# A graph layer's last edges: one run of six groups, or two groups after each of three mixing products

## The chip, the cores and the metric

The kernel runs on one core of a Trainium2 chip (trn2). The metric is the device time of one execution in microseconds (us); the time before is the median of three runs. One further execution was recorded by the hardware profiler, and every view below is of that one.

## The reference

One layer over a graph of 10000 nodes with 512 features and 160000 edges sorted by their target (`dst`), all in float32:

```
xn = layernorm(x)
gnn = relu(segment_sum((xn @ W)[src] * edge_weight, dst) + bias)
q, k, v = xn @ w_qkv.T                 # 8 heads of 64
q = softmax(q, over features) / 8 ; k = softmax(k, over nodes)
mix = layernorm(concat_heads(q @ (k.T @ v)) @ w_out.T) * gamma
x = x + gnn + mix
t = layernorm(x)
router: mean over nodes -> 11 logits -> top 2 -> weight of each of 6 experts
x = x + sum_e weight_e * (gelu(t @ W1_e + b1_e) @ W2_e + b2_e)
```

## The kernel before

The nodes go in 20 chunks (`NCH`): 19 of 512 nodes and a last one, number 19, of 272. A chunk lies on up to 128 partitions, r, with four nodes (`SUB`) on each; a product of the matmul engine takes one of the four, s = 0 to 3. The last chunk has r = 68.

**Edges.** Since segment_sum is linear, the kernel sums normalised rows first and multiplies by W after. `edges_in` (L573) lets GpSimd (POOL) gather rows of the source nodes, 128 at a time, by an indirect DMA (L584), and has VectorE (DVE) make the matrix `sel` that places and weighs them (L590, L592). `edges_summed` (L596) does four matmuls of 128x32 by 128x512 on TensorE (PE, L602) into a PSUM tile `pm` of a pool with two buffers, lets ScalarE (ACT) copy it into `part` (L605, three buffers), and starts a DMA of 256 KB from ACT's queue to `part_d` in memory (L606). In this part of the kernel, that is one group of edges: four gathers, four matmuls, one copy, one DMA. `edges_to(n)` (L689) does groups until n are done, issuing gathers until more than `ahead` tiles of 128 edges are held (`LATE`, 4, in this part); `work(us)` and `put_out` spread groups between products by a pace. There are `NQ` groups in all. Now and then `carry` (L673, issue at L674) adds the second half of some windows' sums to the next window's by one accumulating DMA on POOL's queue.

**Rows.** `attention(c)` (L1041) computes the mixing branch of chunk c: four products `po` (called by `times`, L209), a copy of each to `ot` (L1055) on ACT, statistics, and two DVE steps that finish it. It runs three chunks ahead (`MIXED`). The loop over the chunks then gathers the summed rows (`gathered`, L1016, an indirect DMA on POOL at L1020, which needs the edges of these rows and their carry), transposes them on PE (`pt`, L201) with copies on ACT (`aT`, L203), multiplies by W (`pg`, L209), adds bias and relu and the mixing branch on DVE (L1104, L1105), stores the rows (`x_d`, L1106) from SyncE's (SP's) queue, and takes statistics.

**The tail.** The change stands at c = 17, the third chunk from the end. There `all_edges_in` (L1006) finishes the edges that are left: six groups, one after the other. It then issues the last carry, closes the edges' pools, issues the loads of the first chunk for the experts (`rows_in(0)`, L328, four DMAs on SP) and of the experts' weights (three small ones on ACT's queue, and 17 on SP, L305 and L306). The gathers for chunks 18 and 19 follow, and then attention for chunk 19: products s = 0, 1, 2, then by `beside()` the 16 transposes of chunk 17, then s = 3. Because the pools of the edges are closed, `put_out` does nothing there any more. Small products `pst` (L337) and ACT's normalising (L351) prepare the first chunk for the experts, DVE transposes it (L367), and pg of chunks 17, 18 and 19 follow. After chunk 17, `sums_of_weights` has DVE form sums of W1's blocks (L226 to L229), which the experts' first products (`px`, L243) use; these fill the rest of the kernel.

PE runs in the order in which the program is written (`manual_schedule`). The orders of ACT and DVE are set by a scheduler from the dependences. POOL's and SP's instructions stand in one order each, and every engine runs its own in order.

Of the kernel before, what the change touches and what calls it, by code (L numbers as in the profile page):

```python
# [20 lines left out]
SUB = 4  # L21
# [12 lines left out]
PRODUCT = 0.83  # L34
# [22 lines left out]
def gps_layer_kernel(  # L57
# [22 lines left out]
    KB = D // P  # L80
# [16 lines left out]
    NCH = len(chunks)  # L97
# [50 lines left out]
    NQ = -(-NW // GROUP)  # L148
# [239 lines left out]
    with ExitStack() as ph:  # L388
# [184 lines left out]
        def edges_in(i):  # L573

            t0, batch = tiles_of(i)
            n = min(GROUP * batch, NET - t0)
            m = [None] * n
            for j in range(batch):
                four_of = pools["m"].tile([P, GROUP, D], F32, name="msg")
                for h in range(GROUP):  # L580
                    k = h * batch + j
                    if k < n:
                        m[k] = four_of[:, h, :]
                        nc.gpsimd.indirect_dma_start(  # L584
                            out=m[k], out_offset=None, in_=xn_d,
                            in_offset=bass.IndirectOffsetOnAxis(ap=src_sb[:, t0 + k : t0 + k + 1], axis=0))
            sel = pools["w"].tile([P, 2 * GROUP, WIN], F32, name="sel", bufs=6)
            if n < GROUP * batch:
                nc.vector.memset(sel[:, n:, :], 0.0)
            nc.vector.tensor_tensor(sel[:, :n], iota_w[:, None, :].to_broadcast([P, n, WIN]),  # L590
                                    place[:, t0 : t0 + n, None].to_broadcast([P, n, WIN]), ALU.is_equal)
            nc.vector.tensor_tensor(sel[:, :n], sel[:, :n],  # L592
                                    w_sb[:, t0 : t0 + n, None].to_broadcast([P, n, WIN]), ALU.mult)
            return batch, m, sel
# [89 lines left out]
        done = [0, 0.0]  # L684
# [4 lines left out]
        def edges_to(stop):  # L689
            while done[0] < stop:  # L690
                i = done[0]
                while sum(len(m) for _, m, _ in held["edges"]) <= ahead[0] and i + len(held["edges"]) < NQ:
                    held["edges"].append(edges_in(i + len(held["edges"])))
                edges_summed(i, *held["edges"].pop(0))
                done[0] += 1
                while carried and carried[0][0] == i:
                    carried.pop(0)[1]()

        def work(us):

            done[1] += us
            if not pools:

                normal_rows(int(done[1] / EARLY_TOTAL * (NCH + 1)) + 4 - len(normal))
                return
            edges_to(groups_of(int(done[1] / pace[0])))
# [150 lines left out]
        for c, (_, r) in enumerate(chunks):  # L857
# [31 lines left out]
            else:  # L889
# [4 lines left out]
                for s in range(SUB // 2):  # L894
                    first = seven(ek, qt, s, r, xnT, xs, (wk, wq), kq_sum, lambda n: work(n * KH * PRODUCT))
# [110 lines left out]
        def all_edges_in():  # L1006
            edges_to(NQ)
            carry(CARRIES[-1], NW - 1)
            assert not carried
            pools.clear()  # L1010
            edge_ctx.close()
            io_f["in"] = ctx.enter_context(tc.tile_pool(name="f_in", bufs=1, reuse_waits="tile"))
            held["first_rows"] = rows_in(0)
            experts_weights()

        def gathered(c):  # L1016
            r = chunks[c][1]
            n_rows = far_enough(c)
            at = io.tile([P, SUB, D], F32, name="at", tag="at" if c < NCH - 1 else "qT")
            nc.gpsimd.indirect_dma_start(  # L1020
                out=at[:r].rearrange("p s d -> p (s d)"), out_offset=None, in_=by_four[: n_rows // SUB, :],
                in_offset=bass.IndirectOffsetOnAxis(ap=row_of[:r, c : c + 1], axis=0))
            return at
# [11 lines left out]
        def put_out(us):  # L1035
            if pools:
                work(us)

        ats = []

        def attention(c, beside):  # L1041


            r = chunks[c][1]
            qT, xt = held.pop("last") if c == NCH - 1 else (queries_in(c), rows_again(c))
            ot = io.tile([P, SUB, D], F32, name="ot", bufs=MIXED + 2)
            for s in range(SUB):
                if s == SUB - 1:
                    beside()
                po = psum.tile([P, D], F32, name="po", tag="ps")  # L1050
                times(po, qT, s, r, mix)
                put_out(KB * PRODUCT)
                if c == s == 0:
                    ats.append(gathered(0))
                nc.scalar.copy(ot[:r, s, :], po[:r, :])  # L1055
            mv = small.tile([P, SUB, 2], F32, name="mv")
            row_stats(ot, r, mv)
            for s in range(SUB):
                nc.vector.scalar_tensor_tensor(ot[:r, s, :], ot[:r, s, :], mv[:r, s, 0:1],
                                               gamma_b[:r], op0=ALU.subtract, op1=ALU.mult)  # L1060
                nc.vector.scalar_tensor_tensor(ot[:r, s, :], ot[:r, s, :], mv[:r, s, 1:2],
                                               xt[:r, s, :], op0=ALU.mult, op1=ALU.add)
            return ot

        mixed = [attention(c, lambda: None) for c in range(MIXED)]
        for c, (_, r) in enumerate(chunks):
            ot, at = mixed.pop(0), ats.pop(0)
            aT = io.tile([P, KB, SUB * P], F32, name="aT", bufs=1)

            if c == NCH - 3:  # L1070
                all_edges_in()
                ats += [gathered(c + 1), gathered(c + 2)]

            def nodes_rows():
                transposed(aT, at, r, psum, "ps", by_act=range(KB))

            if c + MIXED < NCH - 1:
                mixed.append(attention(c + MIXED, nodes_rows))
            elif c == NCH - 3:
                mixed.append(attention(NCH - 1, nodes_rows))  # L1080
            else:
                nodes_rows()
            if c < NCH - 3:
                ats.append(gathered(c + 1))
            if c == NCH - 4:
                held["last"] = queries_in(NCH - 1), rows_again(NCH - 1)

            if c == NCH - 3:
                io_f["squares"] = io_f["in"].tile([P, P // SQ, P], F32, name="squares")
                for b in range(P // SQ):  # L1090
                    nc.vector.tensor_copy(
                        io_f["squares"][:, b].rearrange("k (g t) -> k g t", t=SQ),
                        ident[:, None, b * SQ : (b + 1) * SQ].to_broadcast([P, P // SQ, SQ]))
                xn = held.pop("first_rows")
                st = small.tile([P, P // SQ, 1, SUB, 2], F32, name="st_sq", bufs=1)
                stats_of_squares(st, 0)
                for step in normalising(0, xn, st[:, :, 0]):
                    step()
                turn = turned_in(0, rows_turned(0, xn))
            for s in range(SUB):  # L1100
                po = psum.tile([P, D], F32, name="pg", tag="ps")
                times(po, aT, s, r, wg)
                put_out(KB * PRODUCT)
                nc.vector.tensor_tensor(po[:r, :], po[:r, :], bias_b[:r], ALU.add)  # L1104
                nc.vector.scalar_tensor_tensor(ot[:r, s, :], po[:r, :], 0.0, ot[:r, s, :], op0=ALU.max, op1=ALU.add)  # L1105
            nc.sync.dma_start(x1_d[c], ot[:r])  # L1106
            mv = stats2[:, c]
            row_stats(ot, r, mv)

            if c == NCH - 1:  # L1110
                normalize(wg, ot, r, mv)

            nc.vector.scalar_tensor_tensor(mv[:r, :, 0], mv[:r, :, 0], -1.0, mv[:r, :, 1],
                                           op0=ALU.mult, op1=ALU.mult)
            if c < NCH - 1:
                for s in range(SUB):
                    nc.vector.scalar_tensor_tensor(xsum[:r], ot[:r, s, :], mv[:r, s, 1:2], xsum[:r],
                                                   op0=ALU.mult, op1=ALU.add)
                moved = small.tile([P, 1], F32, name="moved")
                nc.vector.tensor_reduce(moved[:r], mv[:r, :, 0], axis=AX.X, op=ALU.add)  # L1120
                nc.vector.tensor_tensor(msum[:r], msum[:r], moved[:r], ALU.add)
            if c == NCH - 3:
                sums_of_weights()
# [350 lines left out]
```

## Time and profile before

| | us |
|---|---|
| median of 3 runs | 3495.81 |
| lowest and highest | 3495.39, 3496.99 |
| profiled execution | 3479.47 |
| its span (first to last instruction) | 3477.7 |
| PE busy | 3259.1 |
| DVE busy | 1764.0 |
| POOL busy | 1323.8 |
| ACT busy | 831.0 |
| mean granted TensorE clock | 0.968 of full speed |

Times in a trace are counted from the first instruction, so the profiled execution ends at 3477.7. An engine's busy time is the sum of its instructions; what matters for a change is which engine waits, where, and for whom. "x24" behind a line of the timeline counts instructions as the profiler records them: a float32 matmul of the program has two records, so a group of edges (four matmuls) is x8, and a product of four matmuls is also x8. The number in brackets is idle time just before, with the instruction that ended it by the semaphore events ("issue" is none that the profile shows, "remote" one that it cannot name).

### The profile page before, as it was taken

To read this page: it belongs to the slowest core of one execution; us is meant where nothing else is said; L and a number is where in the kernel's file an instruction comes from. 1 tells how busy PE (TensorE), PEld (TensorE's weight loads), DVE (VectorE), ACT (ScalarE), POOL (GpSimd) and SP (SyncE) were. 2 spreads that over 40 slices of the span, in tenths; PEclk is the share of its full clock that TensorE was granted. 3 is DMA by queue.
4 is the path that set the end of the run, shared out by engine and by line. 5 is a ranking of instruction groups with operands and counts; after the bars stand their busy time and mean duration, and the time that the engine had idled before them with its cause. 6 is when DMAs were issued, how large, how long until landed. Compare 5 with 4: busy or idle time off the path is not lost. (4 is left out here: it accounts for less than half of the span.)

```text
span 3477.7 us, 35221 instructions
## 1 busy us (share of the span) xinstructions
PE 3259.1 (94%) x12819; PEld 1917.7 (55%) x12819; DVE 1764.0 (51%) x3902; ACT 831.0 (24%) x1674; POOL 1323.8 (38%) x1421
## 2 busy tenths in 40 slices
PE   6899999998999889999999989999999999999998
PEld 3343433333333333333333336888888888888886
DVE  6654544444445435555555557455445445544542
ACT  5322211121122112222221223222222222222221
POOL 3366666666666657767767630000000000000000
PEclk9999999999999979999999999999999999999999
DMA  9677777777767879989899882122121212212111
GB/s 389 239 224 250 226 251 251 256 225 225 239 218 246 256 278 324 322 313 323 312 321 326 291 256 72 53 81 58 52 85 49 61 54 80 57 53 84 50 38 38
DMA packets 216728, 654.33 MB, mean 188 GB/s; under 512 B 34425, under 2 KB 74361, under 8 KB 188831
## 3 DMA queue, kind: packets, MB, share of 16 engines
q0 software_dynamic: 104096, 354.29, 32.2%
q1 hardware_dynamic: 69992, 175.33, 15.3%
q10 hardware_dynamic: 42452, 122.31, 9.2%
q8 instruction: 105, 1.72, 0.2%
q14 instruction: 83, 0.68, 0.1%
HBM read 491.21 MB, written 166.63 MB: 189 GB/s over the span
## 5 line engine op out<-in xcount | busy, mean ns | idle before, releaser
L584 POOL DMA_INDIRECT msg<-xn_d,src_sb x1250 | 1241.6, 993 | 611.0 <-issue 333.9
L602 PE MATMUL pm<-msg,sel 128*32 128x512 f32 x2504 | 356.1, 616 | 40.2 <-issue 34.3
L209 PE MATMUL po<-G,qT 128*128 128x512 f32 (+1 forms) x640 | 305.9, 616 | 24.7 <-issue 23.2
L912 PE MATMUL pc<-xn,ek 128*128 128x512 f32 (+1 forms) x640 | 309.4, 634 | 10.5 <-issue 7.7
L209 PE MATMUL pg<-wq,aT 128*128 128x512 f32 (+1 forms) x640 | 296.4, 608 | 9.7 <-issue 9.0
L605 ACT COPY part<-pm 128x512 f32<-128x512 f32 x217 | 127.0, 585 | 712.7 <-remote 254.6
L209 PEld LDWEIGHTS po<-G,qT 128*128 128x128 f32 (+1 forms) x640 | 117.7, 192 | 202.7 <-issue 195.5
L602 PEld LDWEIGHTS pm<-msg,sel 128*32 128x32 f32 x2504 | 65.8, 110 | 291.9 <-issue 261.1
L209 PEld LDWEIGHTS pg<-wq,aT 128*128 128x128 f32 (+1 forms) x640 | 115.1, 188 | 190.4 <-issue 177.8
L912 PEld LDWEIGHTS pc<-xn,ek 128*128 128x128 f32 (+1 forms) x640 | 125.7, 204 | 170.0 <-issue 158.5
L243 PE MATMUL px<-xnT,w_sb 128*128 128x256 f32 (+1 forms) x800 | 203.2, 377 | 9.1 <-DVE u L1291 9.0
L243 PE MATMUL p<-kq_sum,xs_b 128*128 128x512 f32 (+1 forms) x432 | 201.2, 600 | 2.7 <-issue 2.4
L243 PE MATMUL px<-w_sb,hh 128*128 128x256 f32 (+1 forms) x800 | 185.7, 379 | 0.0
L243 PE MATMUL py<-xs,w_sum 128*128 128x256 f32 (+1 forms) x800 | 185.0, 374 | 0.0
L166 DVE BATCH_NORM_STATS2 st<-ot 128x6 f32<-128x512 f32 (+1 forms) x160 | 110.1, 689 | 137.6 <-issue 74.3
L243 PE MATMUL py<-w_sum,hh 128*128 128x256 f32 (+1 forms) x800 | 179.2, 379 | 0.0
L590 DVE TENSOR_TENSOR sel<-iota_w,place 128x128 f32<-128x128 f32 (+2 forms) x217 | 74.5, 344 | 194.5 <-remote 74.2
L243 PEld LDWEIGHTS px<-xnT,w_sb 128*128 128x128 f32 x800 | 149.5, 191 | 32.5 <-DVE u L1291 13.0
L243 PEld LDWEIGHTS px<-w_sb,hh 128*128 128x128 f32 (+1 forms) x800 | 150.0, 188 | 22.7
L243 PEld LDWEIGHTS py<-w_sum,hh 128*128 128x128 f32 (+1 forms) x800 | 150.0, 188 | 22.7
L243 PEld LDWEIGHTS py<-xs,w_sum 128*128 128x128 f32 x800 | 149.4, 190 | 19.6
L243 PE MATMUL p<-wk,xnT 128*128 128x512 f32 (+1 forms) x288 | 142.7, 618 | 18.4 <-issue 16.3
(298 smaller groups left out, 4589.5 us busy)
## 6 DMA issues: line engine op xcount, KB each, us to landing
part_d<-part ACTq DMA_DIRECT2D x217, 256.0 KB
msg<-xn_d,src_sb POOLq DMA_INDIRECT x1250
xn<-in_x SPq DMA_DIRECT2D x19, 1024.0 KB
xn_d<-xn ACTq DMA_DIRECT2D x19, 1024.0 KB
qT_d<-qT ACTq DMA_DIRECT2D x19, 1024.0 KB
qT<-qT_d SPq DMA_DIRECT2D x19, 1024.0 KB
xt<-in_x SPq DMA_DIRECT2D x19, 1024.0 KB
x_d<-ot SPq DMA_DIRECT2D x19, 1024.0 KB
```

What stands on the lines that cost most here:

```text
L166: nc.vector.bn_stats(st[:r, s, :], t[:r, s, :])
L209: nc.tensor.matmul(po[:r, :], t[:, kb, s * r : (s + 1) * r], w[:, kb, :], start=kb == 0, stop=kb == KB - 1)
L243: nc.tensor.matmul(o, lhs[j], rhs[j], start=start and j == 0, stop=stop and j == n - 1, skip_group_check=True)
L584: nc.gpsimd.indirect_dma_start(out=m[k], out_offset=None, in_=xn_d, in_offset=bass.IndirectOffsetOnAxis(ap=src_sb[:, t0 + k : t0 + k + 1], ...
L590: nc.vector.tensor_tensor(sel[:, :n], iota_w[:, None, :].to_broadcast([P, n, WIN]), place[:, t0 : t0 + n, None].to_broadcast([P, n, WIN]), ...
L602: nc.tensor.matmul(pm[h * WIN : (h + 1) * WIN, :], sel[:, k, :], m[k] if k < len(m) else m[0], start=j == 0, stop=j == batch - 1, skip_gro ...
L605: nc.scalar.copy(part, pm)
L912: nc.tensor.matmul(pc, ek[:r, s, cb * P : (cb + 1) * P], xn[:r, s, :], start=s == 0, stop=s == SUB - 1)
```

## The change

`attention` gets a third argument, `between`. Without it nothing is different. With it, `put_out` is left out and `between(s)` is called after products 0, 1 and 2. At c = 17, for chunk 19's attention, `between` is `late_edges`, which does a third of the groups of edges that are left (two of the six) each time; and the transposes ahead of product 3 are preceded by what is left of `all_edges_in` (the last carry, the closing of the pools, the loads for the experts) and by the gathers of chunks 18 and 19.

```diff
-        def attention(c, beside):
+        def attention(c, beside, between=None):
...
                 times(po, qT, s, r, mix)
-                put_out(KB * PRODUCT)
+                if between is None:
+                    put_out(KB * PRODUCT)
+                elif s < SUB - 1:
+                    between(s)
...
-            if c == NCH - 3:
-                all_edges_in()
-                ats += [gathered(c + 1), gathered(c + 2)]
-
             def nodes_rows():
                 transposed(aT, at, r, psum, "ps", by_act=range(KB))
 
             if c + MIXED < NCH - 1:
                 mixed.append(attention(c + MIXED, nodes_rows))
             elif c == NCH - 3:
-                mixed.append(attention(NCH - 1, nodes_rows))
+                first = done[0]
+
+                def late_edges(s):
+                    edges_to(first + -(-(NQ - first) * (s + 1) // (SUB - 1)))
+
+                def end_of_edges():
+                    all_edges_in()
+                    ats.extend([gathered(c + 1), gathered(c + 2)])
+                    nodes_rows()
+
+                mixed.append(attention(NCH - 1, end_of_edges, late_edges))
```

The instructions are the same, in number and kind. On PE the order of this stretch was: six groups of edges, po s0, s1, s2, transposes of chunk 17, po s3. It is now: po s0, two groups, po s1, two groups, po s2, two groups, transposes of chunk 17, po s3. The orders of POOL and SP are the same as before. On ACT the copies of po and of the edges' sums alternate in the same manner, the DMA of the last group's sums stands behind the first copy of chunk 17's transposes, and the copies of chunk 18's transposes stand behind, instead of ahead of, the root of chunk 17's statistics. On DVE some statistics of chunk 19 stand earlier, and the transposing of the first normalised rows and the sums of the weights stand some steps later.

## The prediction

> **What bounds the kernel now.** I read the page first. TensorE (PE) is busy for 94% of the span, so a change can only win what PE waits, and only near the place that it touches.
>
> ```profile
> span 3477.7 us, 35221 instructions
> PE 3259.1 (94%) x12819; PEld 1917.7 (55%) x12819; DVE 1764.0 (51%) x3902; ACT 831.0 (24%) x1674; POOL 1323.8 (38%) x1421
> PEclk9999999999999979999999999999999999999999
> ```
>
> The other 218.6 us are idle, and the question is how much of it lies where the last groups of edges stand. PE's timeline there (start, us, engine, line, operation, tiles, count, and in brackets the idle time before it and what ended it) shows one hole of 9.52 us and nothing else:
>
> ```profile
> 2012.71 14.00 PE L209 MATMUL pg<-wq,aT 128*128 128x512 f32 x32
> 2026.64 1.92 PE L602 MATMUL pm<-msg,sel 128*32 128x512 f32 x16
> 2029.45 1.06 PE L602 MATMUL pm<-msg,sel 128*32 128x512 f32 x8 [0.89 <-issue]
> 2040.04 4.78 PE L602 MATMUL pm<-msg,sel 128*32 128x512 f32 x24 [9.52 <-issue]
> 2044.75 10.52 PE L209 MATMUL po<-G,qT 128*68 128x512 f32 x24
> 2055.10 1.91 PE L201 MATMUL pt<-ident,at 128*128 128x128 f32 x16
> 2056.85 3.60 PE L209 MATMUL po<-G,qT 128*68 128x512 f32 x8
> 2060.28 0.95 PE L337 MATMUL pst<-stats,squares 128*128 128x8 f32 x8
> 2061.09 13.98 PE L209 MATMUL pg<-wq,aT 128*128 128x512 f32 x32
> 2074.91 1.91 PE L201 MATMUL pt<-ident,at 128*128 128x128 f32 x16
> 2090.39 1.16 PE L201 MATMUL pt<-ident,at 68*128 68x68 f32 x16
> ```
>
> (The timeline counts each matmul of a group twice over its passes: x8 is one group of edges, x24 three.) Call the last six groups g5 to g10 after their order in the tail. g5, g6 and g7 run by 2030.5, PE waits to 2040.0, g8 to g10 follow, then chunk 19's three mixing products. POOL's timeline says what the hole waits for: one gather of messages each 1.25 us, the last of them for g10, and after the edges the carry and the two gathers of summed rows.
>
> ```profile
> 2036.22 0.94 POOL L584 DMA_INDIRECT msg<-xn_d,src_sb  x1 [0.30 <-issue]
> 2051.73 0.96 POOL L674 DMA_DIRECT2D part_d<-part_d  x1 [14.56 <-DMA rw_sb<-in_router_t]
> 2057.30 1.23 POOL L1020 DMA_INDIRECT at<-part_d,row_of  x1 [4.61 <-DMA part_d<-part_d]
> 2058.82 1.12 POOL L1020 DMA_INDIRECT at<-part_d,row_of  x1 [0.30 <-issue]
> ```
>
> From the trace's landing events: the gather issued at 2036.22 has landed by 2040.11. ScalarE's (ACT's) timeline shows a second cause of the same hole: the copy of g6's sums, whose matmuls ended at 2028.6, starts only at 2039.40, so the semaphore updates of PE came late while the gathers flowed, and both buffers of the edges' PSUM were held.
>
> ```profile
> 2028.82 0.59 ACT L605 COPY part<-pm 128x512 f32<-128x512 f32 x1 [15.41 <-issue]
> 2039.40 0.59 ACT L605 COPY part<-pm 128x512 f32<-128x512 f32 x1 [10.00 <-remote]
> ```
>
> The table of windows (us, then busy time of PE, PEld, DVE, ACT and POOL, PE's granted clock, DMA share, GB/s) shows what the hole costs beside itself: the clock is 0.50 and 0.59 after it.
>
> ```profile
> 2035.00:2040.00 5.00, 0.00 (x0) 0.00 (x0) 0.00 (x0) 0.60 (x2) 1.86 (x2) 0.50 0.79 286
> 2040.00:2045.00 5.00, 4.96 (x25) 1.14 (x26) 3.95 (x12) 1.95 (x5) 0.00 (x0) 0.59 0.68 210
> ```
>
> **What is moved, and the direct gain.** The order of PE's instructions becomes: pg of chunk 16, po s0, g5 g6, po s1, g7 g8, po s2, g9 g10, the 16 transposes of chunk 17, po s3, pst, pg of chunk 17. No instruction of POOL or SyncE (SP) changes place. Three po products are 10.52 us and need only chunk 19's queries, whose load was issued at 1933.06 and landed within 5 us. Laid from 2026.64: s0 to 2030.1, g5 and g6 (1.92 us) to 2032.0, s1 to 2035.4, g7 and g8 to 2037.4, s2 to 2040.8, g9 and g10 to 2042.7. The gathers allow it: g8's were issued by 2026.21 and g10's last landed at 2040.11. So the products fill the hole; g10 ends at 2042.7 instead of 2044.8, and what follows it on PE is the transposes, no longer three products. pst, at 2060.28 before, would start at 2042.7 + 1.8 + 3.5 = 2048.0: 12.3 us sooner. Of these 10.5 are the covered products, and 1.9 the clock: 24 edge matmuls took 4.78 us in the slow window, while 16 took 1.92 at full clock, so 24 would take 2.88.
>
> If PE's semaphores again reach ACT late, g7's buffer comes free only near 2039.4; then s2 and g9, g10 are left behind g7, g8, PE idles some 4 us before g7, and pst moves by about 7 us rather than 12.3. I take 12.3, since the first product now gives PE something else to signal, and keep 7 as a bound.
>
> **Where the stall goes.** The next late thing is the summed rows of chunk 18. Their gather was issued at 2057.30 and has landed at 2069.24 (11.95 us); PE used them at 2074.91, so the slack was 5.67 us. This gather stands behind the carry on POOL, and the carry behind the DMA of g10's sums: issued at 2045.51, landed 2049.72, the carry issued 2051.73, landed 2057.03. Of this chain only the head moves. g10 ends 2.1 us sooner; on ACT its copy (0.59 us) is now followed by the first copy of chunk 17's transposes (about 0.5 us) ahead of its DMA. I take 2.1 - 0.5 - 0.2 = 1.4 us; it can be -1 (late semaphores) to +3 (no slow clock and a quicker carry). The rows then land at 2067.85. PE reaches them at 2074.91 - 12.3 = 2062.6 and waits 5.2 us; with the bound of 7 us it reaches them at 2067.9 and waits not at all. In both, the gain at these transposes is 5.67 + 1.4 = 7.1 us: the twelve are won and five given back.
>
> A stall of 5.2 us has its own price, by the rows above: after the hole of 9.52 us the slow clock cost 1.9 us. I take 2.0 us, between nothing (a wait under 4 us) and 2.8 (the whole slow stretch of some 6 us filled with matmuls). The Trainium skill, TensorE: Matmul & The Clock Gate, Part 1, says that about 3.4 us of idle PE suffices to halve the clock, for at least that long; by it alone a wait of 5.2 us starts cold and loses about 1.7 us, so the rule speaks against the change here, and this estimate would make the gain 0.3 us larger than mine.
>
> Chunk 19's rows landed at 2082.35 and were needed at 2090.39. With issue 1.4 us sooner and PE 5 us sooner, 8.04 + 1.4 - 5.1 = 4.3 us of slack are left: hidden.
>
> The orders of ACT and DVE change as well. On ACT the four copies of chunk 18's transposes stand behind the root (0.21 us) of chunk 17's statistics, which waits for DVE; DVE has the time that PE waits for the rows, so I cost this at nothing; without that cover it is up to 1.5 us. On DVE the last two sums of the experts' weights (1.47 us each) come one step later, the last behind the add of the last pg product, and PE's first experts' product waits for such a sum. That is 0.4 to 2.9 us there; but 5 us further on PE waits in any case for u (2.45 us in before, ended by DVE's L1291), and DVE comes earlier to all of it. I take 0.3 us. Statistics of chunk 19 come earlier and the transposing of the first normalised rows (2.30 us) later than pg's adds, which takes work out of PE's way; nothing.
>
> **The sum.** 7.1 - 2.0 - 0.3 = 4.8 us sooner. The profiled execution took 3479.47 us (1.8 beside its span) and would take 3474.7; the median of the timed runs was 3495.81, 16.3 us or 0.47% above it, with the same program, so the difference is carried over unscaled: 3491.0.
>
> **Rivals.**
> *The rows land sooner (faster by more than 0.2%).* Earlier gathers of the same kind took 5.2 to 10.1 us from issue to landing; only the one for chunk 18 took 12 and chunk 19's 23.5, while SP loaded the experts' weights. Issued at 2055.9 and landed after 8 us, the rows are there at 2063.9, PE waits 1.3 us, the clock stays up, and the gain is 11.0 - 0.3 = 10.7: 3485.1. For it: DMA is only at 0.66 to 0.68 share from 2040 to 2050. Against it: SP's loads start when the gathers have landed, so they also move little, and the same transfers meet. The Trainium skill, DMA: Bandwidth & Descriptors, in Queues, rings and completion order, says that a DMA engine takes turns between its queues packet by packet, which would make the gather share with those loads again and stands for the forecast; no row here splits that share.
>
> *The rows land later (slower).* The gather of chunk 18 goes at the pace of chunk 19's, since weights and the first four row loads are now crowded against it. Issued at 2055.9 and 23.5 us on the way, it lands at 2079.4: 4.5 us later than it was needed, and after an idle PE of 17 us the slow clock takes 2 and the sums 0.3: 6.8 slower, 3502.6. It decides from a flight of 16.7 us on (2055.9 + 16.7 + 2.3 = 2074.9). For it: 23.5 us did happen 1.5 us behind. Against: that gather had only 68 rows and queued behind this one.
>
> *Nothing moves.* The late semaphores hold g5 and g7 in turn, g10 ends near 2047, the chain to the rows moves 2 us the wrong way, and the gain is 5.67 - 2 - 2.3 = 1.4: 3494.4. That the change does not do what it says is excluded by the order of the instructions.
>
> **How the numbers follow.** 0.2% is 7.0 us, about what a measurement of this kernel can tell from no change. Forecast (gain 2.0 to 7.0): 0.40. Rows sooner (7.0 to 12.3): 0.35. Nothing moves (within 2 us of no change): 0.10. Rows later, or a wait on ACT, DVE or the rows that I have not found: 0.15. So faster 0.35; same 0.40 + 0.10, less 0.02 for a clock that drifts against it = 0.48; slower 0.17. The range goes from the full 12.3 us (3483.5) to 5.2 slower (3501.0), which leaves out less than one in five, most of it above; the likeliest case by itself is 3488.8 to 3493.8.
>
> **What would show it.** Right: PE without idle from 2026 to 2049 or so, PEclk 1.00 there, g10's matmuls before 2044, the carry issued near 2050, and a new idle of 3 to 5 us before chunk 18's transposes, followed by a PEclk near 0.6. Wrong: a hole that remains before g7 with ACT's copies "remote" (late semaphores); the transposes of chunk 18 without a wait (rows sooner); a gather that flies over 16 us (rows later); an idle before chunk 19's transposes or before the first px longer than the one that I allow.

## The result, and the profile after

| | before, median | after, median | ratio of the mean times (95% interval) |
|---|---|---|---|
| first comparison, 22 runs of each | 3497.2 us | 3503.52 us | 1.0008 (0.9993 to 1.0024) |
| second comparison (below), 23 and 12 runs | 3283.0 us | 3283.21 us | 1.0001 (0.9989 to 1.0012) |

No change that can be measured: both intervals hold 1. The first leaves room for 2.4 us faster to 8.4 us slower. The second comparison and its neighbours ran at a level 6% lower, the kernel before with them, so times are compared only within one. The profiled execution of after has a span of 3510.3 us, against 3477.7 before, but the spans scatter: a second profile of each kernel has 3469.3 (before) and 3479.3 (after). Much of that scatter is older than the change: the last message gather, ahead of which hardly anything is different, goes out at 2036.2 and 2023.0 us before, at 2059.3 and 2029.5 us after. So the spans do not tell what the change does. The tail does, read in parts.

PE's timeline of after, from the end of chunk 16's products (columns as before: start, us, instruction, idle time before it and what ended it; some rows between are left out):

```profile
2050.87 3.60 PE L209 MATMUL po<-G,qT 128*68 128x512 f32 x8
2054.40 1.92 PE L602 MATMUL pm<-msg,sel 128*32 128x512 f32 x16
2056.25 3.65 PE L209 MATMUL po<-G,qT 128*68 128x512 f32 x8
2063.96 3.62 PE L602 MATMUL pm<-msg,sel 128*32 128x512 f32 x16 [4.06 <-ACT part L605]
2067.51 3.65 PE L209 MATMUL po<-G,qT 128*68 128x512 f32 x8
2071.09 1.93 PE L602 MATMUL pm<-msg,sel 128*32 128x512 f32 x16
2072.94 1.97 PE L201 MATMUL pt<-ident,at 128*128 128x128 f32 x16
2078.18 0.95 PE L337 MATMUL pst<-stats,squares 128*128 128x8 f32 x8
2097.60 3.12 PE L201 MATMUL pt<-ident,at 128*128 128x128 f32 x16 [4.63 <-DMA at<-part_d,row_of]
2100.51 14.43 PE L209 MATMUL pg<-wq,aT 128*128 128x512 f32 x32
2130.52 1.10 PE L243 MATMUL px<-xs,w_sum 128*128 128x256 f32 x4 [0.84 <-DVE w_sum L228]
2138.13 1.13 PE L243 MATMUL px<-xnT,w_sb 128*128 128x256 f32 x4 [2.19 <-DVE u L1300]
2139.10 3.48 PE L337 MATMUL pst<-stats,squares 128*128 128x80 f32 x16
2142.38 2.01 PE L243 MATMUL px<-xs,w_sum 128*128 128x256 f32 x4
```

The end of it before, where the first px waits for nothing (rows left out here too):

```profile
2105.12 1.03 PE L243 MATMUL px<-xs,w_sum 128*128 128x256 f32 x4
2112.92 1.13 PE L243 MATMUL px<-xnT,w_sb 128*128 128x256 f32 x4 [2.45 <-DVE u L1291]
2113.88 1.90 PE L337 MATMUL pst<-stats,squares 128*128 128x80 f32 x16
2115.62 1.07 PE L243 MATMUL px<-xs,w_sum 128*128 128x256 f32 x4
```

The order is the announced one, and the idle of 9.52 us has become 4.06. Counted from the end of chunk 16's products (2026.64 before, 2050.87 after):

| start of | before | after | difference |
|---|---|---|---|
| pst | 33.64 | 27.31 | -6.33 |
| transposes of chunk 18 | 48.27 | 46.73 | -1.54 |
| products of chunk 18 | 50.02 | 49.64 | -0.38 |
| first px | 78.48 | 79.65 | +1.17 |

So 6.3 us were won and given back in three places: a wait of 4.63 us for chunk 18's rows; behind it transposes of 3.12 instead of 1.91 us and products of 14.43 instead of 13.90; and a wait of 0.84 us for a sum of the weights ahead of px. In the table pst is the first one, at 2078.18. In the windows of after (us, busy time of PE, PEld, DVE, ACT, POOL, granted clock, DMA share, GB/s) the clock is low after the hole of 4.06 us, after the wait of 4.63 us, and after the two waits of 0.84 and 2.19 us:

```profile
2060.00:2065.00 5.00, 1.04 (x8) 0.18 (x9) 0.30 (x1) 1.17 (x2) 1.12 (x1) 0.90 0.46 137
2065.00:2070.00 5.00, 5.00 (x20) 1.25 (x15) 1.62 (x3) 1.75 (x3) 0.00 (x0) 0.75 0.79 248
2100.00:2105.00 5.00, 5.00 (x14) 2.57 (x13) 2.83 (x9) 1.07 (x2) 0.00 (x0) 0.84 1.03 244
2140.00:2145.00 5.00, 5.00 (x19) 4.49 (x19) 1.67 (x5) 1.98 (x5) 0.00 (x0) 0.50 1.04 180
```

POOL's timeline of after: the last message gather, the carry, the gathers of chunks 18 and 19.

```profile
2059.31 1.82 POOL L584 DMA_INDIRECT msg<-xn_d,src_sb  x1 [0.31 <-issue]
2078.05 0.96 POOL L674 DMA_DIRECT2D part_d<-part_d  x1 [16.92 <-DMA b_sb<-in_b_a]
2085.38 1.03 POOL L1020 DMA_INDIRECT at<-part_d,row_of  x1 [6.38 <-DMA part_d<-part_d]
```

The carry starts 18.74 us after the last message gather, the gather of chunk 18 another 7.33 us later. Before it was 15.51 and 5.57. This chain is 5 us longer, and it is the one that PE waits for.

ACT's timeline shows the late semaphores that the prediction kept as a bound: g5's and g6's matmuls end at 2056.3, and the copy waits until the last message gather lands (its landing events are dated 2063.1 to 2063.6). PE's own semaphore events agree: counted in order, those of these eight matmuls are dated 2060.4 to 2063.5, where the second run of after has them within 1.3 us of the matmuls' ends.

```profile
2063.32 0.58 ACT L605 COPY part<-pm 128x512 f32<-128x512 f32 x1 [6.53 <-remote]
```

### The profile page after: what moved, and what is told of

Read it like the earlier page. It is cut to its first block, busy times and chain, and to the rows that moved or that the text cites. A ratio compares the mean times of both kernels' runs of the same rounds, so it can differ in the third digit from the quotient of the medians.

```text
span 3510.3 us, 35224 instructions
## 1 busy us (share of the span) xinstructions
PE 3252.6 (93%) x12819; PEld 1919.2 (55%) x12819; DVE 1764.7 (50%) x3902; ACT 829.5 (24%) x1674; POOL 1320.1 (38%) x1421
## 5 line engine op out<-in xcount | busy, mean ns | idle before, releaser
L602 PE MATMUL pm<-msg,sel 128*32 128x512 f32 x2504 | 348.9, 611 | 32.1 <-issue 19.9
L243 PE MATMUL px<-xnT,w_sb 128*128 128x256 f32 (+1 forms) x800 | 204.2, 378 | 11.0 <-DVE u L1300 10.8
```

What stands on the lines that cost most here:

```text
L243: nc.tensor.matmul(o, lhs[j], rhs[j], start=start and j == 0, stop=stop and j == n - 1, skip_group_check=True)
L602: nc.tensor.matmul(pm[h * WIN : (h + 1) * WIN, :], sel[:, k, :], m[k] if k < len(m) else m[0], start=j == 0, stop=j == batch - 1, skip_gro ...
```

## The experiments

Times below are us after the issue of the last message gather, read from each profile; there is one profile in each row, so a difference of a few us between two rows can be scatter. "End of 16" is the end of chunk 16's products; it says how far PE is when the gathers end, which differs from run to run. "Gather of 18" has the issue of chunk 18's gather and its last landing event; "wait" is PE's idle ahead of chunk 18's transposes, "on" the time from px to PE's first idle over 0.6 us behind the third chunk of the experts, and the last column the sum of px and on: the whole tail.

| kernel | end of 16 | last sums' DMA | gather of 18: issued, landed | wait | px | on | tail |
|---|---|---|---|---|---|---|---|
| before | -9.5 | 9.3 | 21.1, 33.0 | 0 | 68.9 | 575.3 | 644.2 |
| before again | -3.6 | 10.2 | 20.9, 33.3 | 0 | 69.9 | 576.8 | 646.7 |
| after | -8.3 | 14.7 | 26.1, 38.2 | 4.63 | 71.2 | 581.1 | 652.3 |
| after again | -2.4 | 14.7 | 29.1, 39.0 | 5.43 | 72.3 | 580.2 | 652.5 |
| after, timed | -12.8 | 7.3 | 18.6, 31.5 | 4.99 | 65.4 | 579.2 | 644.6 |
| rows of 18 early | -3.9 | 13.3 | 19.4, 27.6 | 0 | 65.7 | 580.5 | 646.2 |
| weights late | -11.6 | 13.4 | 22.9, 29.0 | 0 | 67.7 | 575.8 | 643.5 |
| edges sooner | 0.0 | 15.7 | 26.7, 38.9 | 2.92 | 75.2 | 575.9 | 651.1 |
| products first | -14.3 | 7.6 | 24.0, 35.8 | 7.84 | 69.2 | 580.9 | 650.1 |
| sums sooner | -6.9 | 12.7 | 27.1, 37.0 | 5.44 | 69.5 | 579.9 | 649.4 |
| three repairs | -11.7 | 7.5 | 13.4, 20.2 | 0 | 58.0 | 583.6 | 641.6 |
| three repairs, timed | -12.3 | 6.6 | 9.6, 19.9 | 0 | 57.3 | 579.8 | 637.1 |
| sums on POOL | -12.9 | 7.0 | 7.9, 17.8 | 0 | 56.8 | 579.1 | 635.9 |
| before, sums on POOL | -12.2 | 5.9 | 16.8, 29.4 | 0 | 71.6 | 573.5 | 645.1 |

**Both kernels again**, unaltered.

> The changed kernel, unaltered, for the scatter of the stretch from the issue of the last message gather to the first experts' product. In the profiles at hand it is 68.9 us before and 71.2 us after. Theory of the rows (chunk 18's summed rows set the end of the stretch: PE reaches its transposes early and waits for them): again a wait of 3 to 6 us ended by the gather of the rows ahead of chunk 18's transposes, a slow clock behind it, and 69 to 73 us. Rival of chance (the two profiles differ by what runs scatter): no such wait, and a stretch under 66 us.

> The kernel before, unaltered, for the same scatter. Theory of the rows: the hole of 7 to 10 us after the third of the last six groups is there again, no wait ahead of chunk 18's transposes, and the stretch is 67 to 71 us. Rival of chance: the stretch is over 73 us, or has no hole.

The wait, its cause and the slow clock behind it came again, at 5.43 us. In this run the semaphores were in time and PE had no hole at all: pst starts 21.5 us after the end of chunk 16's products, as the prediction had laid it out (2048.0 - 2026.6 = 21.4). Nothing was won by it, since the rows landed at 39.0. Before again had a hole of two pieces, 2.27 and 2.58 us, less than the 7 to 10 expected, so the time to be filled is itself not the same in every run; its px, at 69.9, is within the expected 67 to 71.

**Chunk 18's rows ready early.**

```diff
-           (17, 788), (18, 820)]
+           (17, 788), (18, 820), (19, 852)]
...
                 def end_of_edges():
+                    ats.append(gathered(c + 1))
                     all_edges_in()
-                    ats.extend([gathered(c + 1), gathered(c + 2)])
+                    ats.append(gathered(c + 2))
                     nodes_rows()
```

> The changed kernel with chunk 18's rows made ready before the last groups: one more entry (19, 852) in the list of rows at hand, so that the carry is split in two, and the gather of chunk 18 stands behind the first part of it, which needs the edges only up to the third of the last six groups. Theory of the rows: the wait ahead of chunk 18's transposes falls from 4.6 us to 0 to 1, the slow clock behind it goes, and the stretch is 64 to 67 us; chunk 19's rows may then be late by up to 3 us. Rival of order and clock (the late sums of the weights and DVE's order eat the gain downstream): the wait goes, but the stretch stays within 1.5 us of 71.2.

PE's timeline of it:

```profile
2059.35 1.91 PE L201 MATMUL pt<-ident,at 128*128 128x128 f32 x16
2062.89 14.00 PE L209 MATMUL pg<-wq,aT 128*128 128x512 f32 x32 [1.63 <-ACT aT L203]
2092.93 1.10 PE L243 MATMUL px<-xs,w_sum 128*128 128x256 f32 x4 [1.30 <-DVE w_sum L228]
```

The wait for rows is gone, no slow clock follows, and px comes 5.5 to 6.6 us sooner than in the two runs of after: up to px the rows were the limit. Two new waits stand in its place, 1.63 us for ACT's copies (which now stand behind chunk 17's root) and 1.30 for a sum of the weights. Behind px nothing improved (580.5), so the whole tail, 646.2, is better than after's and still no better than before's.

**The experts' weights loaded later.**

```diff
             held["first_rows"] = rows_in(0)
-            experts_weights()
...
             nc.sync.dma_start(x1_d[c], ot[:r])
+            if c == NCH - 3:
+                experts_weights()
```

> The changed kernel with the loads of the experts' weights (20 DMAs) issued behind the store of chunk 17's rows instead of ahead of the last gathers. If the flight of chunk 18's gather (12 us) is long because it shares the DMA engines with these loads, it falls to 5 to 8 us, and the wait ahead of chunk 18's transposes from 4.6 us to under 1; the weights then arrive later and may hold the first experts' product. If the flight is the gather's own, it stays at 11 to 12 us and so does the wait.

POOL's and PE's timelines of it:

```profile
2059.14 0.96 POOL L674 DMA_DIRECT2D part_d<-part_d  x1 [16.83 <-DMA b_sb<-in_b_a]
2064.24 1.03 POOL L1019 DMA_INDIRECT at<-part_d,row_of  x1 [4.14 <-DMA part_d<-part_d]
...
2073.58 1.91 PE L201 MATMUL pt<-ident,at 128*128 128x128 f32 x16
2077.11 14.00 PE L209 MATMUL pg<-wq,aT 128*128 128x512 f32 x32 [1.63 <-ACT aT L203]
```

Two of the 17 loads on SP still went out early, at 15.9 and 16.5; the others began at 34.3, when the rows had landed. The gather flew for 6.14 us instead of 12.09 and 9.90, that of chunk 19 for 10.4 instead of 22.9, the carry gave way after 5.1 instead of 7.3, and the wait is gone. So the loads for the experts account for some 4 to 6 us of the flight. They came later for it, and px waited 3.24 us for a sum. The loads are not all of it: in the runs with the rows early the gathers, issued before most of the loads, flew for 6.8 to 10.3 us.

**How the six groups are spread.** Two groups, then four, then none behind the products; or all six behind the third product.

```diff
-                    edges_to(first + -(-(NQ - first) * (s + 1) // (SUB - 1)))
+                    edges_to(first + 2 if s == 0 else NQ)          # edges sooner
+                    edges_to(NQ if s == SUB - 2 else first)        # products first
```

> The changed kernel with the last four groups of edges together behind the second product, and none behind the third. In the changed kernel the DMA of the last group's sums goes out 14.7 us after the issue of the last message gather, in the kernel before 9.3 and 10.2 us. Theory of the chain (the products now stand ahead of the edges that the carry and the rows of chunk 18 wait for): without the third product ahead of it the DMA goes out at 11 to 12 us, the rows land 2.5 to 4 us sooner, PE's wait ahead of chunk 18's transposes falls from 4.6 and 5.4 us to 1 to 2.5, and the stretch to the first experts' product from 71.2 and 72.3 to 66 to 69 us. Rival (the carry and the gather are slow because of what else the DMA engines move, whatever their start): the wait stays above 4 us.

> The kernel of after with all six groups in one run behind the third product, so that the products stand ahead of the edges as a whole. Theory of the chain: PE has no hole, and the six groups end after three products and six groups from the end of chunk 16's products, as in the changed kernel: the last DMA at 12 to 15 us, the rows late again with a wait of 3 to 6 us, the stretch 70 to 73 us. Rival (it is the alternation of products and edges, with two PSUM buffers held by late semaphores, that delays the last group): the DMA goes out before 11 us, and the stretch is under 69 us.

The first is inconclusive: PE was late in that run (end of 16 at 0.0), so the last DMA went out at 15.7, not 11 to 12, and the wait of 2.92 lies between the two expectations; part of it is that a copy of sums waited 2.68 us for one of the three `part` buffers. The second answers against my chain as I had drawn it: the last DMA went out at 7.6, sooner than before's, and still the gather was issued only at 24.0 and the wait was the longest of all, 7.84 us. Two things make this up. PE was early in that run (end of 16 at -14.3): counted from there the DMA goes out after 21.9 us, against 23.0 in after, so this order of the groups did not bring it forward. And the gather does not follow the sums at a fixed distance: 16.4 us from one to the other here, 10.8 to 11.8 before. The sums' DMA and the carry took 5.8 and 8.4 us to land here, 4.2 and 5.3 before. That SP's loads for the experts, which went out from 13.5 on, slow the carry as they slow the gather is likely from the experiment above, but was not tried in this order.

**The sums of the weights sooner on DVE.**

```diff
+                if c == NCH - 1 and s >= 1:
+                    behind(added, held["sums"])   # order alone: add after the last sum
```

> The changed kernel with one order forced on DVE: the sums of the experts' weights ahead of the adds of the last chunk's products 1 to 3. Behind the first experts' product the changed kernel has two idles close together (0.84 us for a sum and 2.19 us for u) and then the halved clock for 6.8 us, and it takes 580 to 581 us to the third chunk's first wait where the kernel before takes 575 to 577. Theory of the order (this is a loss of its own, made by the late sums): the 0.84 us are gone, the halved clock behind u is gone or half as long, and the 580 become 575 to 578. Rival (chance of the clock): 580 or more.

```profile
2092.18 1.03 PE L243 MATMUL px<-xs,w_sum 128*128 128x256 f32 x4
2100.62 1.13 PE L243 MATMUL px<-xnT,w_sb 128*128 128x256 f32 x4 [3.09 <-DVE u L1302]
2101.58 3.40 PE L337 MATMUL pst<-stats,squares 128*128 128x80 f32 x16
```

The wait for the sum is gone, the wait for u has grown from 2.19 to 3.09, the clock halves for 6.8 us as before it (pst 3.40 us, 1.90 at full clock), and the way on is 579.9, outside the 575 to 578 of the theory and next to the 580 of the rival. So the order of the sums is not a loss of its own; whether chance of the clock has a part, as the rival says, one run does not tell.

**Three repairs together**: the rows early, the sums sooner, and on ACT the copies of chunk 18 ahead of chunk 17's root.

```diff
+                if c == NCH - 2:
+                    behind(roots[-1], copied)     # order alone: root after chunk 18's last copy
```

> The changed kernel with three repairs: chunk 18's rows ready before the last groups (as in the experiment of that name), the sums of the weights ahead of the last chunk's adds, and on ACT the copies of chunk 18's transposes ahead of the root of chunk 17's statistics. In the first of these experiments chunk 18's products waited 1.6 us for these copies and px 1.3 us for a sum. Theory (the three are the whole of the loss, and the products' time is then won): no idle over 1 us between chunk 17's transposes and px, a stretch of 62 to 64 us, and 575 to 578 us from px on to the wait that stands at 580. Rival (DVE is full and sets the end of the stretch): 65 us or more, with waits for DVE.

PE stands without an idle from chunk 17's products to chunk 19's transposes (0.98 us there), and px comes at 58.0, sooner than I had expected and 10.9 us sooner than before (the end of 16 being 2.2 us sooner of that). Then it waits for u, with the clock halved for 10.2 us (the first 2.0 of them in the wait), and the way on is 583.6:

```profile
2108.75 2.07 PE L246 MATMUL px<-xnT,w_sb 128*128 128x256 f32 x4 [4.50 <-DVE u L1308]
```

The rival was right for that half.

**The sums on POOL.** The repairs for rows and root, and W1's sums on the idle POOL (`sums_of` takes the engine as a last argument); and the kernel before with the sums on POOL alone.

```diff
-                w1_sb[:, :KH, q_half], w1_sb[:, KH:, q_half])
+                w1_sb[:, :KH, q_half], w1_sb[:, KH:, q_half], nc.gpsimd)
```

> The changed kernel with chunk 18's rows ready before the last groups, chunk 18's copies ahead of chunk 17's root on ACT, and the sums of the experts' weights moved from DVE to POOL, which is idle there. With the same two repairs and the sums on DVE, PE reached px 10.9 us sooner against the last message gather than in the kernel before, and lost it again in 4.5 us of waiting for u, which stands on DVE behind chunk 19's steps, and in a halved clock of 10.2 us behind that. Theory (DVE's work up to u is the floor that PE's gain runs into): without 5.9 us of sums on DVE the wait for u falls to 0 to 2 us, the time from px to the wait that stood at 583.6 us falls to 574 to 578, and the kernel is 5 to 12 us faster than before. Rival (POOL is too slow for these sums, or slows DVE's own instructions): px waits for a sum by more than 2 us, or DVE's steps of this stretch take over 10% longer, and the kernel is within 4 us of before.

> The kernel before with nothing but the sums of the experts' weights on POOL, to keep the two parts of the last experiment apart. Theory of the floor: PE is not early in this kernel, so only its wait of 2.45 us for u goes; px stands where it stood (68.9 and 69.9 us behind the last message gather), 572 to 575 us from there to the wait that stood at 575 and 577, and a median within 4 us of before. Rival: POOL's sums alone bring 5 us or more.

Measured: 3276.21 us against 3282.76, ratio 0.9979 (0.9970 to 0.9989); and with POOL's sums alone 3287.56, ratio 1.0011 (1.0002 to 1.0020). The first is the fastest version of this study, within the range expected. But its reason is not the one that I gave: the wait for u stayed at 4.54 us. DVE's and POOL's timelines and the windows of the first kernel:

```profile
1886.11 1.85 DVE L171 TENSOR_SCALAR ve<-stats 128x4 f32<-128x4 f32 x1
1888.44 2.47 DVE L180 TENSOR_TENSOR near<-root 128x4 f32<-128x4 f32 x1
1890.95 0.16 DVE L181 SCALAR_TENSOR_TENSOR near<-near,ve 128x4 f32<-128x4 f32 x1
...
1885.05 2.89 POOL L231 TENSOR_TENSOR w_sum<-w_sum,w_sb 128x1280 f32<-128x1280 f32 x1
1888.02 2.88 POOL L232 TENSOR_TENSOR w_sum<-w_sb,w_sum 128x1280 f32<-128x1280 f32 x1
```

```profile
1896.00:1901.00 5.00, 5.00 (x23) 3.98 (x22) 4.83 (x11) 0.00 (x0) 0.00 (x0) 1.00 0.00 0
1901.00:1906.00 5.00, 1.12 (x6) 0.64 (x4) 4.45 (x13) 1.74 (x3) 0.00 (x0) 1.00 0.47 118
```

Steps that take 0.16 to 0.17 us elsewhere took 1.85 and 2.47 while POOL's sums ran (2.9 us each), and each ended within 0.02 us of a sum's end. That is 4.0 of the 5.9 us which DVE was to save. In the windows before u DVE is busy for 4.83 and 4.45 of 5 us, and in the second of them PE has work for 1.12. The Trainium skill (SBUF — State Buffer, SBUF: two separate sides) says that VectorE and GpSimd have one port pair in common: of a GpSimd instruction and a VectorE instruction that needs the pair, the one that starts first holds it to its end, and the other waits. The two rows agree with that.

The sums on POOL alone made the kernel before slower by 4.8 us, a small loss that the interval just keeps clear of nothing, where at most 4 us either way was expected. There, too, two DVE steps stretched, to 2.47 and 2.73 us, and PE waited 1.21 and 1.88 us for DVE ahead of chunk 19's products, with a halved clock of 3.4 us; the wait for u fell to 0.96 us.

**The changed kernel and the three repairs, timed together.**

> The changed kernel once more, timed beside the one below. In the traces its tail, from the last message gather to the wait of the third chunk of the experts, is 652.3 and 652.5 us long, where the kernel before has 644.2 and 646.7. Theory (the change loses in the tail what the traces show): 3 to 9 us slower than before, a ratio of 1.001 to 1.0028. Rival (the tails of the traces are chance): faster, or within 2 us.

> The changed kernel with the three repairs of order (chunk 18's rows before the last groups, the sums of the weights on DVE ahead of the last adds, chunk 18's copies ahead of the root), all sums on DVE. Its tail took 641.6 us in the first trace, against 652.4 in the changed kernel. Theory: 8 to 12 us faster than the changed kernel in the same call, and 2 to 6 us faster than before. Rival (the repairs only move the wait to u, and nothing is left of them): within 3 us of the changed kernel.

After: ratio 1.0001 (0.9989 to 1.0012), so a loss of 3 us or more, as expected, is not seen; the interval leaves room for at most 4 us. The one tail of after at this level fits: PE reaches it early (end of 16 at -12.8), the last sums go out at 7.3 and the tail is 644.6, though it waits 4.99 us for rows as ever. The loss of some 7 us in the earlier tails may belong to runs in which PE is later against the gathers; that is not shown, since the kernel before was not profiled at this level. The nearest to it is before with the sums on POOL, which is the same up to these sums. It has its end of 16 at -12.2, its last sums at 5.9 and its rows landed at 29.4; in after they come at 7.3 and 31.5. So here, too, the change put the rows of chunk 18 later, by 2 us. Three repairs: 3279.3 against 3283.0 before, 0.9988 (0.9977 to 0.9998); 3.9 us faster than after instead of 8 to 12. So sums on POOL gained little over sums on DVE: the medians stand 6.6 and 3.7 us below before's, with intervals that overlap.

## Why the prediction was right or wrong

By its ratio the time lay in the range (3495.81 x 1.0008 = 3498.6 us; the median of 3503.52 by itself lies 2.5 us above its upper end), and "within 0.2%" was the likeliest class. The gain of 4.8 us (a ratio of 0.9986) lies just below both intervals, so the sum was wrong in size: the time of the products was won in part, and then all of it was given back, not five of twelve.

- *The products fill the hole (12.3 us).* Right in kind, half in size: pst 6.3 us sooner. The bound of 7 us for late semaphores was the value to take. My reason against it (the products give PE something else to signal) failed in the first run: the copies waited as before, until the last gather landed. In the second run it held, but there the hole of before again was only 4.9 us.
- *The rows of chunk 18 end it.* Right in kind: a wait of 4.6 to 5.4 us, forecast 5.2, ended by that gather in every run of after. The size is luck. Counted from the end of chunk 16's products, PE came 6.3 us sooner instead of 12.3, and the rows landed 4.0 us later instead of 1.4 sooner; the two errors cancel.
- *The chain to the rows starts 1.4 us sooner.* The step that failed. It started 5.4 us later against the last message gather (14.65 against 9.29 for the last sums' DMA), and the carry took 7.3 instead of 5.6 us. I had laid the groups from PE's side alone; with a copy held by 6.5 us, or with PE later against the gathers, the last two groups stand behind three products that nobody waited for. At the timed level the head was early (7.3) and the wait was the same, since PE was early too; in products first it was longer still. The stall is therefore no remainder of a sum; up to px it is what takes the gain away (without it px came 5.5 to 6.6 us sooner), and behind px the waits for DVE and the slow clock after them take the rest. The rival "rows land sooner", with a flight of 8 us, never came in the changed kernel (9.9, 12.1 and 12.9 us), only with the loads out of the way (6.14 us); "rows land later" never, at 16.7 us. The 5.2 to 10.1 us that this rival cites for earlier gathers are weak: of the 16 landing events, most of these gathers have fewer than ten in the trace.
- *The slow clock behind the stall (2.0 us).* Right: 1.21 on the transposes and 0.53 on the products, 1.7 together; 2.0 in the second run. The rule cited there gives 1.7, and agrees. But a wait need not be as long as the 3.4 us of that rule, and one under 4 us is not free, as I had it at one end of my bounds: the clock also halved after single idles of 2.4 to 3.1 us (last section).
- *ACT's order (nothing, 1.5 without the cover).* Right on both sides: nothing while the rows are late, 1.63 us as soon as they are not.
- *The sums of the weights (0.3 us).* Too small. They showed as 0.84 us; that and the 2.19 for u stand some 6 us apart, and the clock halves for 6.8 us, which costs 3.4, where before it halved for none or 3.4: pst 3.48 us instead of 1.90, and px and its like 2.01 instead of 1.07. The way from px on is 3.4 to 5.8 us longer (580.2 and 581.1 against 575.3 and 576.8). The clock behind u is 1.7 to 3.4 of that; most of the rest is a wait for DVE some 55 us after px, of 2.85 us in both runs of after and 1.15 and 1.36 before, whose cause is open. I had booked the wait and not what it sets off. The experiment on the sums says that they are only the first thing in the way: behind them u waits for the same DVE.
- *The floor that I did not see.* When all three late things are mended, PE is 10.9 us early at px and waits 4.5 us for u, against 2.45 before, with a slow clock behind; of the 10.9 us the whole tail keeps 2.6 to 5.1. u stands in DVE's order behind every step of chunk 19.

Open: why PE's semaphores reach ACT late while gathers flow. It was seen in several runs, not in the second run of after, and not tried by itself. Open, too, is what sets the distance from the last sums to the gather, which ran from 9.5 to 16.4 us in the kernels whose gather follows all the sums.

## What to carry to other kernels

Work that fills a wait is worth something only if what the longest chain needs is not put behind it: before moving filler ahead of a producer, follow that producer's results through every DMA to the engine that needs them, and start the sum there. Then look for the next engine that becomes full, and price each new short wait with the clock loss that it can set off, not with its length alone. Put bulk loads behind a latency-critical gather, or give the gather a head start, and look at who waits for the loads then (px waited 3.24 us here).

## What the runs showed of the hardware

- Short idles can cost more than their length. The granted clock halved for 3.4, 6.8 and 10.2 us at single idles of 2.79, 3.09 and 4.50 us, for 6.8 us after 0.84 and 2.19 us some 6 us apart, and for 3.4 us only at idles of 4.54 and 4.63 us. After one idle of 2.4 us it did in one run of before and did not in the other; after 1.63 and 2.23 us it did not.
- An indirect gather of 128 rows of 8 KB took 6.14 us with 15 of the 17 loads of weights out of the way, 6.8 to 10.3 us where it was issued ahead of most of them, and 9.9 to 12.9 us beside them. A gather of 68 rows lands in two lots: 12 of its 16 landing events after 11.1 to 13.4 us, four after 20.6 to 22.9 (after); with the loads out of the way 4.0 to 5.0 and 9.5 to 10.4.
- POOL's tensor operations of 2.9 us stretched DVE steps of 0.16 us to as much as 2.73.
